# A four-layer decoder on one core: FFN arms reordered, quantised weights turned at other points, tested tiles loaded ahead

## The chip, the core and the metric

The kernel runs on one core of a Trainium2 chip. A core has five engines with instruction queues of their own: TensorE (PE; its weight loads are listed as PEld), VectorE (DVE), ScalarE (ACT), GpSimd (POOL) and SyncE (SP, which here only issues DMAs). TensorE writes PSUM; the others move and change data between PSUM and the on-chip SBUF. The metric is the device time of one execution in microseconds, the median of three runs. Lower is better.

## The reference, cut to what matters

A decoder of four layers works on x of 8 sequences x 112 tokens x 256 features. Each layer has three sublayers (self-attention, cross-attention to a context, feed-forward network), each added to x after a layer norm:

```python
x = x + _L0_ffn_ref(_layernorm(x, axis=-1), L0_ffn_w_gate, L0_ffn_w_up, L0_ffn_w_down)
...
x = x + _L1_ffn_ref(_layernorm(x, axis=-1), L1_ffn_gate_w, L1_ffn_dyn_gate_w, ...)
...
x = x + _L2_ffn_ref(_layernorm(x, axis=-1), L2_ffn_w1_w, L2_ffn_w1_s, L2_ffn_w2_w, ...)
...
x = x + _L3_ffn_ref(_layernorm(x, axis=-1), L3_ffn_gate_w, L3_ffn_up_w, L3_ffn_down_w, ...)
```

Four of the twelve sublayers matter here. Layer 0's FFN is `down(silu(gate(x)) * up(x))` with int32 weights times 1/127 and 768 hidden features. Layer 1's FFN mixes eight small experts and one fixed one by a router. Layer 2's FFN has scaled weights in five products: `silu(w1 x) * (w2 x)` to 1024 features, two further layers h1 and h2 of 1024 x 1024 with a GELU each, and w3 back to 256. Layer 3's FFN fake-quantises its weights to four-bit floats with a scale for each block of 16; the kernel does that quantisation early, beside layer 2's FFN.

## The kernel before

Tokens are worked on in two halves of four sequences (HB = 4, HT = 448 tokens). `self.x` holds x with tokens on partitions, `self.xn` its normed copy, `self.xnT` the normed copy turned, features on partitions, a half in each part of its last axis. A norm is a generator (`normalise`): four pairs of statistics, three groups of small steps for 1/sqrt, two groups that write `xn`, nine steps in all, so that its VectorE work can be dealt out between other work. `turned` puts one 128-feature block of a half through TensorE's transposes.

**Two arms.** The FFNs of layers 0 and 2 have two bodies each, chosen by a flag on the chip. If the weights are exact in a short format, the arm splits every activation into a rounded high part and the rest (`hThi`, `hTlo`, type fp32r) and multiplies both; in the trace both FFNs take this arm. Within an arm the order of TensorE, VectorE and ScalarE is the order of the code (`manual_schedule`); GpSimd's and SP's queues, and all engines between the sublayers, are ordered by a planner at build time, by its own costs and by when inputs are ready.

**One unit of the gated part** is `gated` (line 587): gate and up products for 128 hidden features and one half, 8 matmuls of 128x448 into a `gu` tile (two of these exist), Silu on ScalarE (L595), the product with the up part on VectorE (L597), then `parts` (L571): the high part on ScalarE (L574), the low part, a subtraction, on GpSimd (L576). Scratch for Silu and for the product comes from four pieces of `xnT` (`spare`).

**Layer 0's arm** (`l0_ffn_arm`, lines 1076 to 1092): for each half, turn the half (`turned_parts`, L583 and L585), six gate units with a norm dealt between them, then for each of the four sequences 12 matmuls of 128x256 (six blocks, two parts) and an addition to x (L1092). Layer 1's attention then turns the first half itself (lines 1232 and 1233), computes queries and keys for it, and norms and turns the second half (`ln_T`).

**Layer 1's FFN** tests on the way whether layer 2's weights are exact. `tested(i)` (lines 1470 to 1476) loads one of 11 tiles of 1 MB through SP, two buffers, and takes the sum of magnitudes of the low half words on ScalarE; it is called in the gate units of the second half, in front of other ScalarE work such as the copy of the turned router weights (wT, L1497).

**Layer 2's arm** (`l2_ffn_arm`, lines 2206 to 2249): eight gate units for each half, then h1 and h2: for each half eight units of 16 matmuls of 128x448 (L444), a GELU (L2228), high and low part. Weights come through a ring of four buffers, loaded by GpSimd's DMA queue. Then for each sequence 16 matmuls of 128x256 with w3 and two VectorE steps (L2244, L2245). Beside h1 and h2 the generator `l3_weights` (lines 2484 to 2533) quantises layer 3's three weight tiles: `rounded(i)` is all VectorE work (block maxima L2496, a maximum over partitions on GpSimd L2503, scaling and rounding in two column halves, L2445 to L2478); `turned(i)` puts the result through TensorE (L2520) and copies it (L2521). One step of the generator is taken after unit 3 of each half of h1 and h2; a step turns tile i-1 and rounds tile i. Layer 3's attention (lines 2368 to 2370) then turns the first half itself, and starts a chain: path logits (`paths`), a sigmoid, a product tree (`tree`), turned nodes.

Of the kernel before, what the change touches and what calls it, by code (L numbers as in the profile page):

```python
# [32 lines left out]
P = 128  # L33
# [346 lines left out]
class _Kernel:  # L380
# [190 lines left out]
    def parts(self, dst, src):  # L571

        nc = self.nc
        nc.scalar.copy(dst[0], src)  # L574
        if len(dst) > 1:
            nc.gpsimd.tensor_tensor(dst[1], src, dst[0].bitcast(F32), ALU.subtract)  # L576

    def turned_parts(self, dst, ps, half):

# [4 lines left out]
            if len(dst) > 1:  # L584
                self.nc.vector.tensor_tensor(dst[1][:, kc, cols], tp, dst[0][:, kc, cols].bitcast(F32), ALU.subtract)  # L585

    def gated(self, ps, wg, wu, cols, src, half, dst, scales):

        nc = self.nc
        gu = self.t(ps, [P, 2, 512], "gu")  # L590
        toks = slice(half * HT, (half + 1) * HT)
        for i, m in enumerate((wg, wu)):
            self.mm(gu[:, i, :HT], [(m[:, k, cols], x[:, k, toks]) for k in range(2) for x in src])
        sg = self.spare()
        nc.scalar.activation(sg, gu[:, 0, :HT], AF.Silu, scale=scales[0])  # L595
        h = self.spare() if len(dst) > 1 else dst[0]
        nc.vector.scalar_tensor_tensor(h, gu[:, 1, :HT], scales[1], sg, ALU.mult, ALU.mult)  # L597
        if len(dst) > 1:
            self.parts(dst, h)

    def l0_attn(self):
        nc, tc, w = self.nc, self.tc, self.w
# [455 lines left out]
    def l0_ffn_arm(self, ctx, exact):  # L1058
        nc, tc = self.nc, self.tc
        one = ctx.enter_context(tc.tile_pool(name="l0f_x", bufs=1))  # L1060
        acts = ctx.enter_context(tc.tile_pool(name="l0f", bufs=2))
        ps = ctx.enter_context(tc.tile_pool(name="ps_l0f", bufs=2, space=PSUM))
        ws = []
        for i, (wi, wf) in enumerate(self.wfs):
            if not exact:
                wf = self.t(one, [P, 1536], f"wf{i}")
                nc.gpsimd.tensor_copy(wf, wi)
            ws.append(wf)
        wg, wu = (x.rearrange("p (k n) -> p k n", k=2) for x in ws[:2])
# [6 lines left out]
        hT = {}  # L1076
        for half in range(2):
            hT = self.many(acts, [P, 6, HT], "hT", exact)
            if half:
                self.turned_parts(xT, ps, 1)  # L1080
            for c in range(6):
                dst = [h[:, c, :] for h in hT]
                self.gated(ps, wg, wu, slice(c * P, (c + 1) * P), xT, half, dst, (scale, scale))
                for _ in islice((norm, following)[half], 2):
                    pass
            drain((norm, following)[half])
            for j in range(HB):
                b = half * HB + j
                pm = self.t(ps, [P, 512], "mm")[:S, :D]
                self.mm(pm, [(h[:, c, j * S : (j + 1) * S], wd[:, c, :]) for c in range(6) for h in hT])  # L1090
                x = self.x[:S, b, :]
                nc.vector.scalar_tensor_tensor(x, pm, scale, x, ALU.mult, ALU.add)  # L1092

    def gate_up(self, ps, wg, wu, cols, half):
        gu = self.t(ps, [P, 2, 512], "gu")
# [48 lines left out]
    def l1_attn(self):  # L1144
# [8 lines left out]
        with ExitStack() as ctx:  # L1153
# [75 lines left out]
                oT = oTs.pop(b)  # L1229
                self.add_to_x(b, self.project(ps, b, [oT[:, c, :] for c in range(4)], wo), bo)  # L1230

            for kc in range(2):
                self.cp(self.xnT[:, kc, :HT], self.turned(self.xn, ps, kc, 0, "mm"))
            for c in range(4):
                for which in range(2):
                    query_key(0, c, which)
# [223 lines left out]
    def l1_ffn(self):  # L1460

        nc, tc, w = self.nc, self.tc, self.w
        with ExitStack() as ctx:
            acts = ctx.enter_context(tc.tile_pool(name="l1f", bufs=1))
            work = ctx.enter_context(tc.tile_pool(name="l1f_w", bufs=2))
            test = ctx.enter_context(tc.tile_pool(name="l1f_t", bufs=2))
            ps = ctx.enter_context(tc.tile_pool(name="ps_l1f", bufs=2, space=PSUM))
            low = self.t(acts, [P, len(self.rings["in_wt"][1])], "low")

            def tested(i):  # L1470
                t = self.t(test, [P, COLS], "t")
                nc.sync.dma_start(t, self.args["in_wt"][i])
                bits = t.bitcast(I16).rearrange("p (n two) -> p n two", two=2)[:, :, 0]
                nc.scalar.activation(
                    self.t(test, [P, COLS], "abs", BF16), bits, AF.Abs, accum_out=low[:, i : i + 1]
                )

            self.ln_T(ps)
            route = self.route(ps, acts)
            gw = next(route)  # L1480
# [698 lines left out]
    def l2_ffn_arm(self, ctx, exact):  # L2179

        nc, tc = self.nc, self.tc
        quant = ctx.enter_context(tc.tile_pool(name="l3w", bufs=1))
        acts = ctx.enter_context(tc.tile_pool(name="l2f", bufs=3))
        pool = ctx.enter_context(tc.tile_pool(name="l2f_w", bufs=4))  # L2190
        ps = ctx.enter_context(tc.tile_pool(name="ps_l2f", bufs=2, space=PSUM))
        w = self.ring("in_wt", pool, 4, F32R if exact else F32)
        l3 = iter(self.l3_weights(quant, ps))
        next(l3)

        def block():
            return self.many(acts, [P, 8, HT], "hT", exact)

        xT = [x.rearrange("p (k n) t -> p k (n t)", n=2)[:, :2, :] for x in block()]
        self.turned_parts(xT, ps, 0)  # L2200
        norm = self.normalise(self.x[:, HB:, :], self.xn[:, HB:, :], n=HB)
        w1, w2 = w("w1", 2), w("w2", 2)
        src = []
        for half in range(2):
            dst = block()
            if half:
                self.turned_parts(xT, ps, 1)
            for c in range(8):
                scales = (self.v("l2f_w1_s", c), self.v("l2f_w2_s", c))
                part = [h[:, c, :] for h in dst]  # L2210
                self.gated(ps, w1, w2, slice(c * P, (c + 1) * P), xT, half, part, scales)
                if not half:
                    for _ in islice(norm, 2):
                        pass
            src.append(dst)
        w.done("w2")
        for n in ("h1", "h2"):
            made = []
            for half in range(2):
                dst = block()  # L2220
                for c in range(8):
                    m = w(f"{n}_{c // 2}", 8)
                    pm = self.t(ps, [P, 512], "mm")[:, :HT]
                    cols = slice((c % 2) * P, (c % 2 + 1) * P)
                    self.mm(pm, [(m[:, k, cols], x[:, k, :]) for k in range(8) for x in src[half]])
                    part = [h[:, c, :] for h in dst]
                    y = self.spare() if exact else part[0]
                    nc.scalar.activation(y, pm, AF.Gelu, scale=self.v(f"l2f_{n}_s", c))  # L2228
                    if exact:
                        self.parts(part, y)  # L2230
                    if half and c % 2:
                        w.done(f"{n}_{c // 2}")
                    if c == 3:
                        next(l3, None)
                made.append(dst)
            src = made
        w3, s3 = w("w3", 8), self.o("l2f_w3_s")
        following = self.normalise(self.x[:, :HB, :], self.xn[:, :HB, :], n=HB)
        for b in range(NB):
            toks = slice((b % HB) * S, (b % HB + 1) * S)  # L2240
            pm = self.t(ps, [P, 512], "mm")[:S, :D]
            self.mm(pm, [(h[:, c, toks], w3[:, c, :]) for c in range(8) for h in src[b // HB]])
            y = self.t(quant, [P, D], "y")[:S]
            nc.vector.tensor_tensor(y, pm, s3[:S, :], ALU.mult)  # L2244
            nc.vector.tensor_tensor(self.x[:S, b, :], self.x[:S, b, :], y, ALU.add)  # L2245
            if b >= HB:
                for _ in islice(following, 3):
                    pass
        drain(following)

    def open_last(self, ctx):
        self.w = self.ring("in_wl", ctx.enter_context(self.tc.tile_pool(name="last", bufs=2)), 2)
# [2 lines left out]
    def l3_attn(self):  # L2255
# [10 lines left out]
        with ExitStack() as ctx:  # L2266
# [101 lines left out]
            for kc in range(2):  # L2368
                self.cp(self.xnT[:, kc, :HT], self.turned(self.xn, ps, kc, 0, "mm"))
            paths(0)  # L2370
            tree(0)
            self.ln_T(ps, 1, "mm")
# [111 lines left out]
    def l3_weights(self, pool, ps):  # L2484
# [38 lines left out]
        sizes = ((2, 8), (2, 8), (8, 2))  # L2523
        loaded(0)
        yield
        for i in range(4):
            if i > 0:
                turned(i - 1, *sizes[i - 1])
            if i < 3:
                rounded(i, *sizes[i])  # L2530
            if i < 2:
                loaded(i + 1)
            yield

    def l3_ffn(self):
# [142 lines left out]
```

## Time and profile before

| | us |
|---|---|
| median of three runs | 2171.72 |
| lowest, highest | 2168.49, 2174.79 |
| the profiled execution's own time | 2168.82 |
| its span, first to last instruction | 2167.0 |
| layer 0's arm, first transpose to last sum's start (TensorE) | 536.60 to 585.28 |
| layer 1's attention, first transpose, first query matmul | 587.14, 589.62 |
| layer 1's FFN, second half's gates to the first sums | 947.6 to 998.2 |
| layer 2's gates, first to last matmul's start | 1627.27 to 1663.71 |
| layer 2's h1 and h2 | 1663.90 to 1782.44 |
| layer 2's results | 1782.65 to 1797.57 |
| layer 3's attention, path logits | 1806.31 |

The mean granted clock of TensorE is 0.946 of full speed. The page gives each engine's busy time and its share of the span, then groups of instructions by line, with their mean time and what ended the idle time before them. A timeline line reads: start in us, length in us, engine, line, operation, what it writes and reads, how many; in brackets the idle time before it and what ended that. "issue" is time in which nothing that the profile shows was waited for. Matmuls are pipelined: a 128x448 one in fp32r is listed with 0.36 us, and at full clock one starts every 0.2 us.

### The profile page before, as it was taken

To read this page: it belongs to the slowest core of one execution; us is meant where nothing else is said; L and a number is where in the kernel's file an instruction comes from. 1 tells how busy PE (TensorE), PEld (TensorE's weight loads), DVE (VectorE), ACT (ScalarE), POOL (GpSimd) and SP (SyncE) were. 2 spreads that over 40 slices of the span, in tenths; PEclk is the share of its full clock that TensorE was granted. 3 is DMA by queue.
4 is the path that set the end of the run, shared out by engine and by line. 5 is a ranking of instruction groups with operands and counts; after the bars stand their busy time and mean duration, and the time that the engine had idled before them with its cause. 6 is when DMAs were issued, how large, how long until landed. Compare 5 with 4: busy or idle time off the path is not lost. (4 is left out here: it accounts for less than half of the span.)

```text
span 2167.0 us, 45439 instructions
## 1 busy us (share of the span) xinstructions
PE 1938.5 (89%) x17912; PEld 1244.4 (57%) x17912; DVE 1386.8 (64%) x3905; ACT 869.0 (40%) x2420; POOL 281.9 (13%) x480
## 2 busy tenths in 40 slices
PE   7999999898898899899899989899998997899844
PEld 3545544465666566545566455556667886566623
DVE  5666666686655677553566676567624866667688
ACT  2444444562212456452033223466525322356532
POOL 1111111001302100000001342100003530100000
PEclk9999999998899999999999999999999997999956
DMA  5000001103000000223101010000022210000000
GB/s 208 3 3 3 3 22 39 33 21 107 1 1 16 21 2 2 79 89 135 40 1 59 1 42 8 1 2 2 1 78 72 98 39 26 1 2 2 2 0 17
DMA packets 11486, 69.20 MB, mean 32 GB/s; under 512 B 1290, under 2 KB 3082, under 8 KB 4874
## 3 DMA queue, kind: packets, MB, share of 16 engines
q1 hardware_dynamic: 9684, 54.69, 7.0%
q0 software_dynamic: 1584, 11.54, 1.5%
q8 instruction: 145, 2.38, 0.4%
q14 instruction: 73, 0.60, 0.1%
HBM read 65.30 MB, written 0.92 MB: 31 GB/s over the span
## 5 line engine op out<-in xcount | busy, mean ns | idle before, releaser
L727 PE MATMUL g<-w,hT 128*32 128x256 f32 x3552 | 236.7, 384 | 1.8 <-DVE hT L757 1.5
L1338 DVE TENSOR_REDUCE xnm<-sc 112x1 f32<-112x375 f32 x384 | 184.6, 541 | 40.0 <-PE sc L444 39.4
L1351 PEld LDWEIGHTS tr<-cst,xe 112*125 112x125 f32 x1152 | 151.5, 188 | 94.6 <-issue 38.1
L1351 PE MATMUL tr<-cst,xe 112*125 112x112 f32 x1152 | 192.9, 289 | 6.8 <-DVE xeT L1359 4.2
L727 PEld LDWEIGHTS g<-w,hT 128*32 128x32 f32 x3552 | 93.2, 109 | 121.8 <-DVE hT L757 83.0
L1357 ACT COPY xeT<-tr 125x336 f32<-125x336 f32 x192 | 85.4, 445 | 158.1 <-PE tr L1351 158.1
L444 PE MATMUL mm<-xnT,w 128*128 128x448 f32 x316 | 136.0, 572 | 9.4 <-DVE qT L1320 2.9
L1359 DVE COPY xeT<-tr 125x336 f32<-125x336 f32 x192 | 97.3, 507 | 68.6 <-PE tr L1351 61.8
L690 PE MATMUL g<-xw,cst 128*32 128x256 f32 x1792 | 137.9, 379 | 0.0
L1342 ACT ACTIVATE xe<-sc,xnm 112x375 f32<-112x375 f32 x256 | 126.6, 582 | 7.3 <-DVE xnm L1338 7.3
L753 ACT ACTIVATE th<-cell 128x64 f32<-128x64 f32 x224 | 57.5, 257 | 144.3 <-DVE cell L749 141.9
L444 PE MATMUL mm<-w,hT 128*112 128x256 f32 x448 | 103.4, 392 | 0.0
L740 ACT ACTIVATE sg<-g 128x192 f32<-128x192 f32 x224 | 74.1, 331 | 67.3 <-PE g L727 45.6
L444 PEld LDWEIGHTS mm<-xnT,w 128*128 128x128 f32 x316 | 60.0, 200 | 67.9 <-issue 44.2
L576 POOL TENSOR_TENSOR hTlo<-xnT,hThi 128x448 fp32r<-128x448 f32 x60 | 74.9, 1256 | 160.8 <-issue 82.7
L444 PE MATMUL mm<-hThi,w 128*128 128x448 f32 x256 | 95.2, 372 | 0.0
L444 PE MATMUL mm<-hTlo,w 128*128 128x448 f32 x256 | 94.7, 370 | 0.0
L444 PEld LDWEIGHTS mm<-w,hT 128*112 128x112 f32 x448 | 81.7, 184 | 21.7 <-issue 3.5
L758 POOL COPY hs<-hT 128x16 f32<-128x16 f32 x224 | 51.8, 231 | 318.4 <-DVE hT L757 318.4
L755 DVE TENSOR_TENSOR h<-sg,th 128x64 f32<-128x64 f32 x224 | 50.5, 226 | 63.9 <-ACT th L753 63.8
L444 PE MATMUL sc<-xkT,qT 32*112 32x375 f32 x768 | 89.8, 519 | 0.0
L1367 PE MATMUL av<-xeT,xv 125*32 125x112 f32 x2304 | 86.4, 266 | 2.1 <-ACT xeT L1357 2.1
(482 smaller groups left out, 3961.9 us busy)
## 6 DMA issues: line engine op xcount, KB each, us to landing
w<-in_w SPq DMA_DIRECT2D x22, 1024.0 KB, 5.0
t<-in_wt SPq DMA_DIRECT2D x11, 1024.0 KB, 4.9
w<-in_wt POOLq DMA_DIRECT2D x11, 1024.0 KB, 5.4
raw<-in_wq SPq DMA_DIRECT2D x3, 1024.0 KB, 5.2
cx<-in_ctx SPq DMA_DIRECT2D x2, 1500.0 KB
wi<-in_wint SPq DMA_DIRECT2D x3, 768.0 KB, 5.6
w<-in_w SPq DMA_DIRECT2D x2, 896.0 KB, 10.7
w<-in_w SPq DMA_DIRECT2D x2, 768.0 KB, 4.1
```

The costliest lines, as they stand in the source:

```text
L444: self.nc.tensor.matmul(out, lhsT, rhs, start=i == 0, stop=i == len(pairs) - 1)
L576: nc.gpsimd.tensor_tensor(dst[1], src, dst[0].bitcast(F32), ALU.subtract)
L690: nc.tensor.matmul(g[32 * j : 32 * j + 32, :], pick[:, t % 16, :], xw[:, l, t // 16, 256 * j : 256 * j + 256], start=True, stop=t == 0, sk ...
L727: nc.tensor.matmul(g[32 * j : 32 * j + 32, :], hT[l][:, c, :], whh[l][:, c, 256 * j : 256 * j + 256], start=False, stop=c == 1, skip_group ...
L740: nc.scalar.activation(sg[:, :192], g[:, :192], AF.Sigmoid)
L753: nc.scalar.activation(th, cell[l], AF.Tanh)
L1338: nc.vector.tensor_reduce(nm, sc, AX.X, ALU.max, negate=True)
L1342: nc.scalar.activation(e, sc, AF.Exp, bias=nm)
L1351: nc.tensor.transpose(tp[:CH, i * S : (i + 1) * S], e[:, i * CH : (i + 1) * CH], self.ident[:S, :S])
L1357: nc.scalar.copy(eT, src)
L1359: nc.vector.tensor_copy(eT, src)
L1367: nc.tensor.matmul(avs[b][32 * j : 32 * j + 32, c * S : (c + 1) * S], values[b % 2][:CH, i, 4 * c + j, :], eTs[b, c, j][:, i, :], start=i ...
```

## The change

Layer 0's arm does all six units of the first half, three of the second, the first half's sums, the other three units (with the norm of the new first half dealt between), then the second half's sums over five blocks for four sequences in four PSUM tiles, the next sublayer's transposes of the first half (`head_T`), and last the sixth block. In both arms the low part of every odd unit is subtracted on VectorE instead of GpSimd (`on`). In layer 2's arm the second half is turned after unit 5 of the first; the first half's results are taken after unit 5 of h2's second half, the next norm in units 6 and 7, `head_T` after the sixth result. The generator for layer 3's weights has rounding and turning as steps of their own, taken at units 0 and 7. Layers 1 and 3's attention lose their own transposes of the first half. Tested tiles have three buffers and are loaded three ahead; the tests' output has one buffer of its own.

```diff
-    def gated(self, ps, wg, wu, cols, src, half, dst, scales):
+    def gated(self, ps, wg, wu, cols, src, half, dst, scales, on=None):
...
-            nc.gpsimd.tensor_tensor(dst[1], src, dst[0].bitcast(F32), ALU.subtract)
+            (on or nc.gpsimd).tensor_tensor(dst[1], src, dst[0].bitcast(F32), ALU.subtract)
...
+    def head_T(self, ps):
+
+        for kc in range(2):
+            self.nc.scalar.copy(self.xnT[:, kc, :HT], self.turned(self.xn, ps, kc, 0))
...
+        for _ in units(0, range(6)):
+            for _ in islice(norm, 2):
+                pass
+        drain(norm)
+        self.turned_parts(xT, ps, 1)
+        for _ in units(1, range(3)):
+            pass
+        for j in range(HB):
+            pm = self.t(ps, [P, 512], "mm")[:S, :D]
+            sums(pm, 0, j, range(6))
+            add(pm, 0, j)
+        for _ in units(1, range(3, 6)):
+            for _ in islice(following, 2):
+                pass
+        pms = [self.t(ps, [P, 512], "mm")[:S, :D] for _ in range(2)]
+        wide = self.t(ps, [P, 2, 512], "gu")
+        pms += [wide[:S, i, :D] for i in range(2)]
+        for j in range(HB):
+            sums(pms[j], 1, j, range(5))
+        drain(following)
+        self.head_T(ps)
+        for j in range(HB):
+            sums(pms[j], 1, j, (5,))
+            add(pms[j], 1, j)
...
-            for kc in range(2):
-                self.cp(self.xnT[:, kc, :HT], self.turned(self.xn, ps, kc, 0, "mm"))
...
-            test = ctx.enter_context(tc.tile_pool(name="l1f_t", bufs=2))
+            test = ctx.enter_context(tc.tile_pool(name="l1f_t", bufs=3))
+            junk = ctx.enter_context(tc.tile_pool(name="l1f_j", bufs=1))
...
+                loaded()
+
+            for _ in range(3):
+                loaded()
...
+                on = nc.vector if c % 2 else nc.gpsimd
+                self.gated(ps, w1, w2, slice(c * P, (c + 1) * P), xT, half, part, scales, on)
                 if not half:
                     for _ in islice(norm, 2):
                         pass
+                    if c == 5:
+                        drain(norm)
+                        self.turned_parts(xT, ps, 1)
...
                 for c in range(8):
+                    if c in (0, 7):
+                        next(l3, None)
...
-                    if c == 3:
-                        next(l3, None)
+                    if n == "h2" and half:
+                        if c == 5:
+                            for b in range(HB):
+                                result(b, made[0])
+                        if c > 5:
+                            for _ in islice(following, 4):
+                                pass
...
         drain(following)
+        for b in range(HB, NB):
+            result(b, src[1])
+            if b == HB + 1:
+                self.head_T(ps)
...
-        for i in range(4):
-            if i > 0:
-                turned(i - 1, *sizes[i - 1])
-            if i < 3:
-                rounded(i, *sizes[i])
+        for i in range(3):
+            rounded(i, *sizes[i])
             if i < 2:
                 loaded(i + 1)
+            yield
+            turned(i, *sizes[i])
             yield
```

More of the change, by code (lines that the diff above doesn't have):

```diff
@@ L569, in spare, with parts @@
         return self.xnT[:, self.turn // 2, (self.turn % 2) * HT : (self.turn % 2 + 1) * HT]
-    def parts(self, dst, src):
+    def parts(self, dst, src, on=None):
         nc = self.nc
@@ L598, in gated @@
         if len(dst) > 1:
-            self.parts(dst, h)
+            self.parts(dst, h, on)
+    def head_T(self, ps):
+        for kc in range(2):
+            self.nc.scalar.copy(self.xnT[:, kc, :HT], self.turned(self.xn, ps, kc, 0))
     def l0_attn(self):
@@ L1075, in l0_ffn_arm @@
         following = self.normalise(self.x[:, :HB, :], self.xn[:, :HB, :], n=HB)
[L1076 to L1092, printed above, removed]
+        hT = [self.many(acts, [P, 6, HT], "hT", exact) for _ in range(2)]
@@ new lines, in units, with sums @@
+        def units(half, cs):
+            for c in cs:
+                dst = [h[:, c, :] for h in hT[half]]
+                on = nc.vector if c % 2 else nc.gpsimd
+                self.gated(ps, wg, wu, slice(c * P, (c + 1) * P), xT, half, dst, (scale, scale), on)
+                yield
+        def sums(pm, half, j, cs):
+            for c in cs:
+                for h in hT[half]:
+                    nc.tensor.matmul(
+                        pm, h[:, c, j * S : (j + 1) * S], wd[:, c, :],
+                        start=c == 0 and h is hT[half][0], stop=c == 5 and h is hT[half][-1], skip_group_check=True,
+                    )
@@ new lines, in add @@
+        def add(pm, half, j):
+            x = self.x[:S, half * HB + j, :]
+            nc.vector.scalar_tensor_tensor(x, pm, scale, x, ALU.mult, ALU.add)
+        for _ in units(0, range(6)):
[9 more added lines that the diff above has]
+            add(pm, 0, j)
@@ L1465, in l1_ffn, with loaded @@
             work = ctx.enter_context(tc.tile_pool(name="l1f_w", bufs=2))
-            test = ctx.enter_context(tc.tile_pool(name="l1f_t", bufs=2))
+            test = ctx.enter_context(tc.tile_pool(name="l1f_t", bufs=3))
+            junk = ctx.enter_context(tc.tile_pool(name="l1f_j", bufs=1))
             ps = ctx.enter_context(tc.tile_pool(name="ps_l1f", bufs=2, space=PSUM))
             low = self.t(acts, [P, len(self.rings["in_wt"][1])], "low")
+            raws = []
+            def loaded():
+                if len(raws) < low.shape[1]:
+                    raws.append(self.t(test, [P, COLS], "t"))
+                    nc.sync.dma_start(raws[-1], self.args["in_wt"][len(raws) - 1])
             def tested(i):
-                t = self.t(test, [P, COLS], "t")
-                nc.sync.dma_start(t, self.args["in_wt"][i])
-                bits = t.bitcast(I16).rearrange("p (n two) -> p n two", two=2)[:, :, 0]
+                bits = raws[i].bitcast(I16).rearrange("p (n two) -> p n two", two=2)[:, :, 0]
                 nc.scalar.activation(
-                    self.t(test, [P, COLS], "abs", BF16), bits, AF.Abs, accum_out=low[:, i : i + 1]
+                    self.t(junk, [P, COLS], "abs", BF16), bits, AF.Abs, accum_out=low[:, i : i + 1]
                 )
+                loaded()
+            for _ in range(3):
+                loaded()
             self.ln_T(ps)
@@ L2205, in l2_ffn_arm @@
             dst = block()
-            if half:
-                self.turned_parts(xT, ps, 1)
             for c in range(8):
@@ L2210, in l2_ffn_arm @@
                 part = [h[:, c, :] for h in dst]
-                self.gated(ps, w1, w2, slice(c * P, (c + 1) * P), xT, half, part, scales)
+                on = nc.vector if c % 2 else nc.gpsimd
+                self.gated(ps, w1, w2, slice(c * P, (c + 1) * P), xT, half, part, scales, on)
                 if not half:
@@ L2214, in l2_ffn_arm, with result @@
                         pass
+                    if c == 5:
+                        drain(norm)
+                        self.turned_parts(xT, ps, 1)
             src.append(dst)
         w.done("w2")
+        s3 = self.o("l2f_w3_s")
+        following = self.normalise(self.x[:, :HB, :], self.xn[:, :HB, :], n=HB)
+        def result(b, src):
+            w3 = w("w3", 8)
+            toks = slice((b % HB) * S, (b % HB + 1) * S)
+            pm = self.t(ps, [P, 512], "mm")[:S, :D]
+            self.mm(pm, [(h[:, c, toks], w3[:, c, :]) for c in range(8) for h in src])
+            y = self.t(quant, [P, D], "y")[:S]
+            nc.vector.tensor_tensor(y, pm, s3[:S, :], ALU.mult)
+            nc.vector.tensor_tensor(self.x[:S, b, :], self.x[:S, b, :], y, ALU.add)
         for n in ("h1", "h2"):
@@ L2232, in l2_ffn_arm @@
                         w.done(f"{n}_{c // 2}")
-                    if c == 3:
-                        next(l3, None)
+                    if n == "h2" and half:
[5 more added lines that the diff above has]
+                                pass
                 made.append(dst)
             src = made
[L2237 to L2248, printed above, removed]
         drain(following)
+        for b in range(HB, NB):
+            result(b, src[1])
+            if b == HB + 1:
+                self.head_T(ps)
     def open_last(self, ctx):
@@ L2366, in result @@
                 self.add_to_x(b, self.project(ps, b, [oT[:, c, :] for c in range(2)], wo))
-            for kc in range(2):
-                self.cp(self.xnT[:, kc, :HT], self.turned(self.xn, ps, kc, 0, "mm"))
             paths(0)
@@ L2525, in l3_weights @@
         yield
-        for i in range(4):
-            if i > 0:
-                turned(i - 1, *sizes[i - 1])
-            if i < 3:
-                rounded(i, *sizes[i])
+        for i in range(3):
+            rounded(i, *sizes[i])
             if i < 2:
                 loaded(i + 1)
+            yield
+            turned(i, *sizes[i])
             yield
```

## The prediction

> **What bounds the kernel now.** I read the page first, then the chain of work that ended last in the stretches that the diff touches, then each engine's timeline there.
>
> ```profile
> PE 1938.5 (89%) x17912; PEld 1244.4 (57%) x17912; DVE 1386.8 (64%) x3905; ACT 869.0 (40%) x2420; POOL 281.9 (13%) x480
> ```
>
> TensorE is busy nearly always, and the change neither adds nor removes a matmul. So only TensorE's idle time in the four touched stretches can be won or lost, and the slow matmuls that follow idle time. The largest such wait is in layer 2's FFN. In the chain there (start, length, piece):
>
> ```profile
> 1704.40 1.15 POOL hTlo L576
> ...
> 1705.79 6.00 issue
> ...
> 1711.86 0.39 POOL gs L2503
> ...
> 1720.17 1.53 DVE wq L2478
> 1721.70 1.07 DVE qs L2445
> 1722.80 3.52 DVE qs L2446
> ...
> 1737.83 1.46 PE tr L2520 x12
> 1739.30 28.20 PE mm L444 x128
> ```
>
> Here rounding matrix 1 on VectorE (1704.69 to 1737.78, 33.1 us) took longer than the 8 units (one half of an h layer) that TensorE had in front of it, and TensorE waited from 1730.1 to 1737.83: 7.7 us. Two things stretch the rounding. GpSimd is gone for 6.00 us ahead of its partition reduction (0.39 us), and VectorE's small steps are held while GpSimd subtracts (L2446 took 3.52 us here, 0.20 where GpSimd was away). VectorE's timeline for matrix 0:
>
> ```profile
> 1665.89 3.72 DVE L2496 TENSOR_REDUCE amax<-raw 128x128 f32<-128x2048 f32 x1
> ...
> 1677.38 0.16 DVE L2504 RECIPROCAL gs<-gs 128x1 f32<-128x1 f32 x1 [7.45 <-POOL gs L2503]
> ```
>
> It ended at 1701.81, 35.9 us after its start, and no one waited: its turning stood at unit 12.
>
> The other waits are short. TensorE in the sums of layer 0's FFN, and at the heads of the layers behind both arms:
>
> ```profile
> 552.93 0.37 PE L444 MATMUL mm<-wf,hThi 128*112 128x256 f32 x1 [0.61 <-ACT hThi L574]
> 554.14 0.37 PE L444 MATMUL mm<-wf,hTlo 128*112 128x256 f32 x1 [0.84 <-POOL hTlo L576]
> ...
> 587.14 0.96 PE L515 MATMUL mm<-cst,xn 112*128 112x112 f32 x8 [1.59 <-DVE st L480]
> ```
>
> ```profile
> 1800.47 0.99 PE L515 MATMUL mm<-cst,xn 112*128 112x112 f32 x8 [2.63 <-DVE y L2244]
> 1806.31 3.21 PE L444 MATMUL mm<-own,xnT 128*112 128x40 f32 x16 [4.85 <-DVE xnT L437]
> ```
>
> **1. Turning the quantised weights: +15.8.** Count TensorE's units of h1 and h2 from 0, 16 matmuls each at 0.2025 us, 3.24 us, unit 0 starting at 1663.90. Before, rounding 0 is issued at unit 3, turning 0 at unit 12, turning 1 at 20, turning 2 at 28. After, the two steps are separate and are taken at c = 0 and c = 7 of each half: rounding 0 at unit 0, turning 0 ahead of unit 7, rounding 1 at unit 8, turning 1 at 15, turning 2 at 23. VectorE has no other work in these units, so rounding 0 cannot start sooner for being issued sooner; its turning stands five units earlier.
>
> Rounding 0, from 1663.90: it started at 2.0; the last unit's subtraction, now on VectorE in front of it, makes that 3.3. Its two reductions take 4.04, so the maximum is ready at 7.35. GpSimd subtracts for unit 0 until 7.27 (1671.17), then is gone 5.8 us and reduces; VectorE goes on at 13.5, as before. The steps left need 16.7 us when nothing holds them (8.6 for the first column half, 1677.38 on, less its two held steps; 8.1 for the second). GpSimd comes back at 20.4 (1684.29) with six subtractions waiting; before, seven took VectorE 6.2 us, so six take 5.3. End: 13.5 + 16.7 + 5.3 = 35.5. TensorE is at unit 7 at 22.9 (1686.8) and in order, so everything behind waits **12.6 us**. After the 7.7 us wait before, 12 transposes and 14 matmuls took 6.4 us where full speed needs 3.5: **2.9** more.
>
> Rounding 1 then finds GpSimd drained, as matrix 2 did before (26.3 us, reduction waited for 0.55): start 37.8, end 64.1; TensorE needs 1.4 + 8 x 3.24 + 2.3 and is at unit 15 at 65.2: no wait, by 1 us. Rounding 2 finds GpSimd just having subtracted, as matrix 1 did before: 67.2 + 33.1 = 100.3, TensorE at unit 23 at 92.0: **8.3**, plus 2.9. Sum 26.7 against 7.7 + 2.9 before, and 0.3 for the four transposes that could run ahead of that wait: +15.8. Bounds: with no gap at the reduction and no held steps rounding 0 lasts 21.3 us, ends at 24.6, and the first wait is 1.7; with none later, the sum is 9 below before. With matrix 1 late as well (33.1 or more), another 6 to 11 above. Where GpSimd's queue puts the reduction is not in the diff; I take the order that the trace shows, by when inputs are ready.
>
> **2. Layer 0's arm: -2.9.** I lay the arm out from its rows: gate unit 8 x 0.2015; Silu 0.55, product 0.62 (L597), high part 0.57, low part 1.15 on GpSimd; a norm 2.2 us of statistics, 2.2 of small steps, 1.5 of scaling. A low part on VectorE has no row; the subtraction L585 of that shape took 0.62. Bounds: 0.2 below (64-element steps) and 1.15 above, if a GpSimd subtraction holds it (L463 took 1.12 instead of 0.16); I take 0.62.
> Gone, counted between issues: the waits in both sums (0.77 + 1.09 + 0.44 + 1.10, twice: 6.8), the half-speed matmuls after them (17 at 0.213 instead of 0.118, twice: 3.2), 1.1 at the half boundary, 0.9 at unit 5 of half 1: 12.0. New: VectorE waits at odd units for the high part, subtracts, and only then takes norm steps, +1.2 in half 0. The transposes of half 1 now come straight behind unit 5: they wait 2.3 for the norm, and the next gates wait 2.1 for casts that stand behind unit 5's on ScalarE (the same order cost 2.4 between issues at 1647.33), 1.6 of half-speed matmuls follow. At the end 1.9 for unit 4's GpSimd part, 0.9 for the next norm, 0.75 for transposes moved in, 0.8 for an even chance of slow matmuls: 11.6. So -0.4 in the arm. Behind it 585.56 to 589.62 (4.06) shrinks to 1.58, as the head's transposes are done: -2.5. Bounds -6 (no slow matmuls) and +2 (the first query evacuations queue behind the other half's 6 us norm).
>
> The Trainium skill (TensorE: Matmul & The Clock Gate, What's actually happening) has the clock fall only after an idle window of about 3.4 us; here 2.2 us idle was followed by 8 slow matmuls (1648.58 on). By the page the boundary would cost 1.6 less; I go by the row. The same skill (SBUF — State Buffer, Who interferes with whom) says that a VectorE instruction with two SBUF inputs and a GpSimd one that reads SBUF block each other; that speaks against half the subtractions on VectorE, and would put the sum about 1 us higher, as an estimate; the L463 row shows such a hold. The sum does not use it.
>
> **3. Layer 2's gates: -0.5.** The same layout with 0.63 and 0.68: half 1's transposes now come behind unit 5 and hide most of the 2.9 us between issues at the boundary, but norm and low parts on VectorE delay half 0 by 1.1 and the transposes by 2.2, and half 1's loop grows 0.1 a unit. Bounds -2 and +1.5 (the slow matmuls stay or not).
>
> **4. Layer 2's end: -3.8.** The first half's results run ahead of unit 6, so the last unit's parts are no longer covered: low part 2.6 us after its matmuls, 1.65 of sums in front, +0.8; transposes +0.8. Behind the arm the path head came 8.46 after the last matmul (1797.85 to 1806.31); now TensorE needs about 2.5. Then z, sigmoid, tree, with VectorE shared with the other half's norm: tree end 17.4 before, about 12 after: -5.4. Bounds -6 and -1 in all (norm last, norm first). w3, now read three units sooner, is issued by GpSimd at unit 1 of that half, lands in 5.4 us and is read at unit 5, 13 us later: nothing.
>
> **5. Tested tiles: -1.3.** TensorE waits 5.20 for wT behind three tests on ScalarE; one of them waited 1.27 for its tile. Three tiles loaded at the start remove that; the rest stays. The other wait (1.56) has no TensorE wait behind it: nothing. The loads are issued by SP in the same places, one more at the start, where the DMA engines are mostly idle; the tests' shared output is written by ScalarE alone, in order, and costs nothing. SP also issues the raw weights, 5.2 us to land, two steps ahead of their use: nothing. Bounds 0 and -2.
>
> **Sum:** 15.8 - 2.9 - 0.5 - 3.8 - 1.3 = +7.3. The profiled execution took 2168.82 (span 2167.0); the median is 2.9 higher. 2171.72 + 7.3 = **2179.0**.
>
> **Rivals.** (a) GpSimd reduces ahead of unit 0's subtraction: its gap starts some 3 us sooner and fewer steps are held, first wait about 7: 2173, within 0.3% (what a measurement here can tell from nothing, 6.5 us). For it: the reduction is issued first now. Against: the trace orders by readiness, and unit 0's part is ready at 6.0, the maximum at 7.35. (b) Rounding 1 is late too, as its margin is 1 us: +11, 2190. (c) Faster: GpSimd's gap is hidden and few steps held in all three roundings, so part 1 is 9 under before, and parts 2 to 5 keep 8.5: 2154. It decides when the three roundings stay below 24 us; the shortest so far was 26.3. (d) It does not do what it says: the weights are not turned later against TensorE, and part 1, at about half of its size, cancels parts 2 to 5: 2171.
>
> **Numbers.** Forecast 0.50 (2174 to 2184, of it 0.10 below 2178.2), (a) 0.18, (b) 0.15, (c) 0.12, (d) 0.05. Faster 0.12, same 0.10 + 0.18 + 0.05 = 0.33, slower 0.40 + 0.15 = 0.55. The range takes in (a), (b) and (d), with part 2's better end: 2165 to 2192.
>
> **What would show it.** TensorE's longest wait in h1 and h2 on the rounded weights (wq, L2478) in front of unit 7 of h1, about 12 us, then none, then about 8. Waits of 2 us on the norm and the casts between layer 0's halves; no waits on hThi or hTlo in its first sums; the attention's first matmul about 1.6 behind the arm. It is wrong if the first wait is under 5 us, or the chain passes elsewhere.

## The result and the profile after

| us | before | after |
|---|---|---|
| median, 14 runs each, on the same chip | 2169.04 | 2174.66 |
| lowest, highest | 2167.29, 2174.79 | 2171.15, 2182.90 |
| the profiled execution, its span | 2168.82, 2167.0 | 2173.44, 2171.5 |
| layer 0's arm, first transpose to first query product | 53.0 | 52.3 |
| layer 2's gates, first matmul to the first of h1 | 36.6 | 34.3 |
| first matmul of h1 to the path logits | 142.4 | 150.0 |

The changed kernel is slower by 0.22% (ratio 1.0022, 95% interval 1.0013 to 1.0031). The forecast was 2179.0 and slower by over 0.3%; the time lies in its range, but in the case "within 0.3%".

The page's busy times of the changed kernel:

```profile
PE 1935.5 (89%) x17912; PEld 1241.9 (57%) x17912; DVE 1389.4 (64%) x3917; ACT 869.4 (40%) x2422; POOL 262.9 (12%) x466
```

The number of matmuls is the same; GpSimd has lost 19 us and 14 subtractions, VectorE has gained 12 instructions. Next the list of TensorE's waits (who waits for whom: us in all, times, longest), the touched ones. Lines of the code have moved: L2529 was L2478, L2571 was L2520.

```profile
PE tr L2571 <- DVE wq L2529: 19.4, 2, 10.1
PE tr L444 <- ACT wT L1537: 4.4, 2, 3.8
```

Before, these were 7.7 (one wait) and 5.8 (longest 5.2). The rounded weights are waited for twice instead of once. VectorE's and GpSimd's timelines show the first rounding:

```profile
1664.62 3.73 DVE L2547 TENSOR_REDUCE amax<-raw 128x128 f32<-128x2048 f32 x1
...
1672.16 0.17 DVE L2555 RECIPROCAL gs<-gs 128x1 f32<-128x1 f32 x1 [3.49 <-POOL gs L2554]
...
1682.35 1.14 DVE L2496 TENSOR_SCALAR qs<-amax,gs 128x64 f32<-128x64 f32 x1
1683.52 1.08 DVE L2497 TENSOR_SCALAR qs<-qs 128x64 f32<-128x64 f32 x1
```

```profile
1662.28 1.14 POOL L576 TENSOR_TENSOR hTlo<-xnT,hThi 128x448 fp32r<-128x448 f32 x1 [0.59 <-ACT hThi L574]
...
1671.74 0.38 POOL L2554 PARTITION_ALL_REDUCE gs<-top  x1 [7.79 <-issue]
1678.88 8.93 POOL L576 TENSOR_TENSOR hTlo<-xnT,hThi 128x448 fp32r<-128x448 f32 x7 [6.76 <-issue]
```

GpSimd goes to the reduction ahead of unit 0's subtraction, is gone 7.79 us before it and 6.76 after it, and comes back with seven subtractions due; beside them five of VectorE's steps of 64 elements take 1.05 to 1.14 us instead of 0.20 to 0.23. The rounding lasts 30.2 us, and TensorE waits:

```profile
1694.89 1.46 PE L2571 MATMUL tr<-ident,wq 128*128 128x128 bf16 x12 [10.09 <-DVE wq L2529]
1696.12 0.72 PE L444 MATMUL mm<-hThi,w 128*128 128x448 f32 x1
1696.64 0.57 PE L444 MATMUL mm<-hTlo,w 128*128 128x448 f32 x1
```

A matmul listed with 0.57 runs at half speed (0.37 us to the next one). TensorE's timeline between layer 0's halves, behind its arm, between layer 2's halves, and at layer 2's end:

```profile
553.37 0.55 PE L515 MATMUL tr<-cst,xn 112*128 112x112 f32 x2 [0.59 <-DVE xn L490]
554.46 1.02 PE L515 MATMUL tr<-cst,xn 112*128 112x112 f32 x6 [0.54 <-DVE xn L490]
556.87 0.74 PE L444 MATMUL gu<-xThi,wf 128*128 128x448 f32 x1 [1.39 <-ACT xThi L583]
```

```profile
585.99 0.27 PE L1093 MATMUL gu<-wf,hTlo 128*112 128x256 f32 x1
589.23 3.33 PE L444 MATMUL mm<-xnT,w 128*128 128x448 f32 x4 [2.96 <-DVE va L455]
```

```profile
1642.09 1.02 PE L515 MATMUL tr<-cst,xn 112*128 112x112 f32 x6 [0.60 <-DVE xn L490]
1642.88 0.45 PE L444 MATMUL gu<-hThi,w 128*128 128x448 f32 x1
```

```profile
1809.92 0.28 PE L444 MATMUL mm<-w,hTlo 128*112 128x256 f32 x1
1811.45 0.75 PE L444 MATMUL mm<-own,xnT 128*112 128x40 f32 x6 [1.24 <-DVE x L2269]
```

Behind waits of 0.56 and 0.60 us ahead of the transposes, the gates of layer 2's second half start without one (before, 2.22 us and half speed behind it). The first query product stands 3.24 us behind layer 0's arm (before 4.3), though its operand is ready; the path logits stand 1.5 us behind layer 2's (before 8.7).

### The profile page after: what moved, and what is told of

It reads as the page before. It is cut to its first block, busy times and chain, and to the rows that moved or that the text cites. A ratio compares the mean times of both kernels' runs of the same rounds, so it can differ in the third digit from the quotient of the medians.

```text
span 2171.5 us, 45439 instructions
## 1 busy us (share of the span) xinstructions
PE 1935.5 (89%) x17912; PEld 1241.9 (57%) x17912; DVE 1389.4 (64%) x3917; ACT 869.4 (40%) x2422; POOL 262.9 (12%) x466
## 5 line engine op out<-in xcount | busy, mean ns | idle before, releaser
L1398 PEld LDWEIGHTS av<-xeT,xv 125*32 125x32 f32 x2304 | 58.6, 109 | 43.1 <-issue 34.6
## 6 DMA issues: line engine op xcount, KB each, us to landing
w<-in_w SPq DMA_DIRECT2D x2, 896.0 KB, 10.8
```

What stands on the lines that cost most here:

```text
L1398: nc.tensor.matmul(avs[b][32 * j : 32 * j + 32, c * S : (c + 1) * S], values[b % 2][:CH, i, 4 * c + j, :], eTs[b, c, j][:, i, :], start=i ...
```

## The experiments

Executions of one kernel differ by several us in code that no edit touched (TensorE falls to half speed at other places), so beside each median stand the stage's times from the profiled execution. "h1 to paths" is from the first matmul of h1 to the path logits. In this stage the same code took 150.0 us (changed), 151.8 (e12) and 152.6 (e6), so a difference under some 3 us there says little by itself. The ratio is to the kernel before, timed beside each run.

| kernel | median | ratio to before, 95% interval | gates | h1 to paths |
|---|---|---|---|---|
| before | 2169.0 to 2169.8 | | 36.6 | 142.4 |
| changed | 2174.66 | 1.0013 to 1.0031 | 34.3 | 150.0 |
| e1, old points | 2160.96 | 0.9951 to 0.9979 | 34.3 | 137.3 |
| e2, before with the new points | 2184.97 | 1.0052 to 1.0091 | 36.7 | 158.6 |
| e3, points 0, 11, 21, 31 | 2160.92 | 0.9940 to 0.9972 | 34.3 | 135.6 |
| e4, no reduction | 2162.59 | 0.9949 to 0.9982 | 34.3 | 138.5 |
| e5, no subtractions in h1, h2 | 2158.35 | 0.9935 to 0.9964 | 34.3 | 132.4 |
| e6, old layer 0 | 2177.31 | 1.0020 to 1.0046 | 34.3 | 152.6 |
| e7, points 0, 11, 22, 31 | 2158.51 | 0.9933 to 0.9959 | 34.3 | 131.6 |
| e8, low parts on GpSimd | 2174.82 | 1.0004 to 1.0031 | 33.2 | 151.2 |
| e9, e7 and e8 | 2156.07 | 0.9928 to 0.9960 | 33.2 | 138.6 |
| e10, before with e7's points | 2172.72 | 1.0007 to 1.0029 | 36.7 | 143.5 |
| e11, old end | 2183.91 | 1.0044 to 1.0070 | 34.3 | 156.3 |
| e12, old boundary | 2181.08 | 1.0040 to 1.0064 | 37.7 | 151.8 |

My theory: the points at which the weights are turned cost about 13 us, everything else gains. The main rival: the points cost little, the loss sits in layers 0 and 1.

**e1: the old points in the changed kernel**, with the old generator, which turns matrix i-1 and rounds matrix i in one step.

```diff
-                    if c in (0, 7):
-                        next(l3, None)
...
+                    if c == 3:
+                        next(l3, None)
```

> The changed kernel with the old points for the quantised weights (one step of the generator after unit 3 of each half; a step turns matrix i-1, then rounds matrix i); all else as changed. Theory T (the turning points cost what the two profiles show: h1 and h2 without the moved results took 118.7 us before and 131.9 after, so 13.2; everything else gains): 2174.7 - 13 = 2161 to 2162, faster than both kernels; one wait of TensorE on the rounded weights, 7 to 8 us, instead of 10.1 and 9.3. Rival R (the turning points cost little on balance, because the slow matmuls and the rounding contention come anyway, and the loss sits in layers 0 and 1): 2170 to 2175.

Measured 2160.96, 13.7 less than the changed kernel, and 12.7 less from h1 to the paths. The rival falls. One wait is left:

```profile
PE tr L2571 <- DVE wq L2529: 7.2, 1, 7.2
```

**e2: the new points in the kernel before.**

```diff
-        for i in range(4):
-            if i > 0:
-                turned(i - 1, *sizes[i - 1])
-            if i < 3:
-                rounded(i, *sizes[i])
+        for i in range(3):
+            rounded(i, *sizes[i])
...
+            yield
+            turned(i, *sizes[i])
...
+                    if c in (0, 7):
+                        next(l3, None)
...
-                    if c == 3:
-                        next(l3, None)
```

> The kernel before with only the new points for the quantised weights (rounding at unit 0, turning at unit 7 of a half, as steps of their own). Theory T: 2169.0 + 13 = 2182 (waits of TensorE on the rounded weights of about 10 ahead of unit 7 of h1 and 9 ahead of unit 7 of h2's first half, each followed by slow matmuls). My prediction on record put this part at +15.8, so 2185. Rival R: 2169 to 2174.

2184.97: 15.2 more than the kernel before, 16.2 in the stage. The recorded +15.8 is near this sum, but not by its terms: TensorE's waits on the rounded weights were 10.10, 0.71 and 9.54 us, where it had 12.6, none and 8.3, and one of 1.53 on the GELU's scratch came on top. That the errors cancel is luck.

**e3: later points**, with the old generator.

```diff
-                    if c in (0, 7):
+                    if (n, half, c) in (("h1", 0, 0), ("h1", 1, 3), ("h2", 0, 5), ("h2", 1, 7)):
                         next(l3, None)
```

> The changed kernel with the generator's steps (turn i-1, round i) at units 0, 11, 21 and 31 of h1 and h2, so that each rounding has 10 or 11 units of TensorE (32 to 36 us) in front of its turning. Theory T (a rounding takes 27 to 35 us of VectorE; a turning less than that behind its rounding is a wait, one that is further behind costs nothing): no wait on the rounded weights, the two waits of 19.4 and about 5 of slow matmuls behind them gone: 2174.7 - 24 = 2151, faster than the kernel before by 18. Rival R2 (three roundings back to back end at about 100 us, where the moved results begin, and VectorE holds their sums): the wait moves there, 2157 to 2163.

2160.92, neither theory's mechanism. The third rounding ended at 1768.4, before the moved results; the second one was late:

```profile
1700.51 3.70 DVE L2547 TENSOR_REDUCE amax<-raw 128x128 f32<-128x2048 f32 x1
...
1711.85 0.16 DVE L2555 RECIPROCAL gs<-gs 128x1 f32<-128x1 f32 x1 [7.32 <-POOL gs L2554]
```

It lasted 38 us (27.2 in the changed kernel, where its reduction was waited for 0.55), and TensorE waited 4.57 for it. In the changed kernel TensorE's own 10 us of standing had left GpSimd without subtractions, so that it had changed over to the reduction in time:

```profile
1701.16 0.38 POOL L2554 PARTITION_ALL_REDUCE gs<-top  x1 [13.35 <-DVE top L2553]
```

With no such wait the change-over came late. The other traces agree: in each kernel that subtracts and reduces, a rounding behind a wait of TensorE of 4.6 us or more waited 0.55 or 0.56 for its reduction, and one behind a shorter wait or none 1.5 to 7.9. My theory took the length of a rounding as a given; it depends on the wait that it causes.

**e4: no reduction.**

```diff
-            nc.gpsimd.partition_all_reduce(gs, top, P, bass_isa.ReduceOp.max)
+            nc.vector.tensor_copy(gs, top)
```

> The changed kernel with the maximum over partitions left out (each partition's own maximum is used, so the scale of the quantised weights is another); a copy of one element a partition on VectorE stands in its place. GpSimd then only subtracts. Theory G (both things stretch a rounding: the wait for the reduction, 3.5, 0.6 and 7.6 us in the three, and small steps held by GpSimd's subtractions): roundings of about 27 us each, the waits of 10.1 and 9.3 shrink to about 6.6 and 2: 2174.7 - 12 = 2163. Rival G2 (the holds come only in a burst when GpSimd returns from the reduction with 6 or 7 subtractions due; without a gap there is no burst): roundings of 22 to 24 us, waits 2 and 0: 2174.7 - 21 = 2154. Rival G3 (VectorE alone sets the length): less than 4 us gained, 2171 or more.

2162.59, waits of 5.48 and 1.31 us: theory G. What is left of the two waits is then to come from the subtractions that hold VectorE, which e5 takes away.

**e5: no subtractions in h1 and h2.**

```diff
                     if exact:
-                        self.parts(part, y)
+                        for d in part:
+                            nc.scalar.copy(d, y)
```

> The changed kernel, but in h1 and h2 the low part is a copy of the whole value on ScalarE (so the products there are other ones) and GpSimd subtracts nothing beside the roundings; it keeps the three maxima over partitions and the weight loads. Theory G (GpSimd pays 6 to 7 us each time it goes from subtractions to the maximum and back, and its subtractions hold VectorE's small steps): with no subtraction between them the second and third maximum are waited for 0.6 us, no step is held, and roundings take about 21 to 22 us where the reduction is not waited for; the two waits of TensorE shrink from 10.1 and 9.3 to at most 3 and 0: 2174.7 - 19 = 2156. Rival G4 (the 6 to 7 us belong to every maximum over partitions by itself, whatever stands before it): the second and third are waited for about 7 us too, roundings of 28 us, waits of about 8 and 3: 2165.

2158.35; waits of 3.97 and none. The second rounding, which waits for nothing, lasts 21.2 us (1691.37 to 1712.55), and no step of 64 elements is held. GpSimd's timeline:

```profile
1672.27 0.38 POOL L2555 PARTITION_ALL_REDUCE gs<-top  x1 [7.90 <-issue]
1695.49 0.35 POOL L2555 PARTITION_ALL_REDUCE gs<-top  x1 [22.84 <-DVE top L2554]
...
1724.28 0.35 POOL L2555 PARTITION_ALL_REDUCE gs<-top  x1 [0.94 <-DVE top L2554]
```

Only the first reduction, behind the gates' subtractions, has the gap; the other two run as soon as VectorE has their input, weight loads between them or not. So the gap ahead of a reduction belongs to the change from subtractions (theory G; G4 falls). The gap on the way back, 6.7 to 7.7 us ahead of the first subtraction behind each reduction, is missing in e4, which has no reduction.

**e6: layer 0's old arm** in the changed kernel.

```diff
-        hT = [self.many(acts, [P, 6, HT], "hT", exact) for _ in range(2)]
...
+        hT = {}
+        for half in range(2):
+            hT = self.many(acts, [P, 6, HT], "hT", exact)
...
+            for kc in range(2):
+                self.cp(self.xnT[:, kc, :HT], self.turned(self.xn, ps, kc, 0, "mm"))
```

> The changed kernel with layer 0's old arm, and layer 1's attention turning its first half itself as before; the rest as changed. My prediction on record put layer 0's part at -2.9, so without it 2177.6. Theory S (the gain in the arm is given back at once: the first query product waits 2.96 us for VectorE behind the arm, and the matmuls behind that wait run at half speed): 2174 to 2175.5. Rival S2 (the new arm is a loss, and the profile of one execution hides it): 2172 or less.

2177.31: 2.7 more, which is the recorded number and not theory S. But the two intervals overlap (1.0013 to 1.0031, 1.0020 to 1.0046), and the profiles give 0.5 up to the first query product (0.7 against the kernel before) and nothing at the attention's next transposes, at 609 us. Between -1 and 6 us is all that the times say.

**e7: e3 with the second turning one unit later.**

```diff
-                    if (n, half, c) in (("h1", 0, 0), ("h1", 1, 3), ("h2", 0, 5), ("h2", 1, 7)):
+                    if (n, half, c) in (("h1", 0, 0), ("h1", 1, 3), ("h2", 0, 6), ("h2", 1, 7)):
```

> The changed kernel with the generator's steps at units 0, 11, 22 and 31. With 0, 11, 21 and 31 it took 2160.9; TensorE waited there 4.57 us ahead of the second turning, and slow matmuls followed. Theory T: one unit (3.24 us) later leaves a wait of 1.3 and no slow matmuls: 2160.9 - 3.3 - 2.5 = 2155, faster than both kernels. Rival R2 (the third rounding then reaches into the moved results and VectorE holds their sums): no gain, 2160 to 2162.

2158.51, faster than both kernels, by less than expected. A wait of 1.36 on the rounded weights is left, 1.45 on the GELU's scratch and 1.48 on the sums:

```profile
1720.45 0.47 PE L444 MATMUL mm<-hThi,w 128*128 128x448 f32 x1 [1.45 <-ACT xnT L2284]
```

**e8: every low part on GpSimd**, in both arms.

```diff
-                on = nc.vector if c % 2 else nc.gpsimd
+                on = nc.gpsimd
```

> The changed kernel with every low part of the two arms on GpSimd, as before; all else as changed. By my prediction VectorE's share of them delays the first half's gates (1.2 us in layer 0, 1.1 in layer 2, and the transposes behind unit 5 by 2.2), against waits for GpSimd at the sums and at the end of the arms. Theory V (the gates gained 2.3 us through the place of the transposes alone, and VectorE's subtractions cost a little): layer 2's gates 33 to 34 us instead of 34.3, time 2173 to 2175. Rival V2 (taking half the subtractions from GpSimd is what keeps the arms free of waits): 2177 to 2180, with waits on the low parts in layer 0's sums of the first half.

2174.82, the same. Layer 2's gates are 1.1 shorter, as theory V has it, and layer 0 to the first query product is 47.8 instead of 52.3; h1 to the paths is 1.2 longer. In e9, with the same low parts, layer 0 takes 48.4; the other kernels with the new arm take 50.9 to 52.7. So by these two profiles the new order of layer 0 gains 4.6 to 5.2 us on the kernel before (53.0), and the low parts on VectorE take most of that away. The medians don't show it: e8's 12 runs spread from 2164 to 2179, and where its 4.5 us are lost again stays open.

**e9: e7's and e8's edits together.**

> The changed kernel with the generator's steps at units 0, 11, 22 and 31 (2158.5 by itself) and every low part on GpSimd (which by itself made layer 2's gates 33.2 us instead of 34.3 and took 2174.8 against 2174.7). Theory V (VectorE's subtractions lengthen the gates by 1.1 us in layer 2 and by about as much in layer 0, and the later first rounding that this brings is now covered): 2158.5 - 2 = 2156 to 2157. Rival: nothing that these runs can tell, 2158 to 2160.

2156.07, the lowest median of all; its interval overlaps e7's, so the time doesn't show theory V. From h1 to the paths it took 7.1 us more than e7 (in an execution whose earlier layers took 13 us less): the sums waited 3.02 us for VectorE and then ran at half speed for 6.1, and a second wait for the scratch was enough for half speed:

```profile
1709.57 0.54 PE L444 MATMUL mm<-hThi,w 128*128 128x448 f32 x1 [1.76 <-ACT xnT L2284]
1709.91 0.58 PE L444 MATMUL mm<-hTlo,w 128*128 128x448 f32 x1
```

**e10: e7's points in the kernel before**; the edit is e7's line in place of `if c == 3`.

> The kernel before with nothing changed but the generator's steps, at units 0, 11, 22 and 31 in place of 3, 12, 20 and 28. Theory T: the wait of 7.7 us and the 2.9 of slow matmuls go, a wait of 1 to 2 stays: 2169.3 - 9 = 2160. With the arms' parts added it took 2158.5, so these would then be worth less than the 8.8 that they showed with the old points. Rival (h1 and h2 last 112.7 us without the moved results there and 118.5 before, so 5.8 and no more): 2163.5.

2172.72, slower than before: the expectation fell, and its rival too. TensorE no longer waits 7.7 us for the rounded weights, but it waits elsewhere:

```profile
1684.65 0.74 PE L444 MATMUL mm<-hThi,w 128*128 128x448 f32 x1 [2.83 <-ACT xnT L2230]
```

```profile
1674.66 0.38 POOL L2503 PARTITION_ALL_REDUCE gs<-top  x1 [8.06 <-issue]
1682.50 7.41 POOL L576 TENSOR_TENSOR hTlo<-xnT,hThi 128x448 fp32r<-128x448 f32 x6 [7.45 <-issue]
```

The GELU writes into one of four scratch pieces, which are free again when GpSimd has subtracted from them. Here GpSimd is back 20.3 us behind the start of h1 (1662.21), when TensorE has done six units; in e7 after 17.3 (1662.75 to 1680.03). With 1.47 more for the scratch, 1.34 and 1.76 for the rounded weights, the 7.7 us are spent again: h1 and h2 last 119.4 us, before 118.5. In e7 the same two rows are:

```profile
1672.60 0.38 POOL L2554 PARTITION_ALL_REDUCE gs<-top  x1 [7.34 <-issue]
1680.03 8.70 POOL L576 TENSOR_TENSOR hTlo<-xnT,hThi 128x448 fp32r<-128x448 f32 x7 [7.05 <-issue]
```

Of the 3.0 us by which GpSimd is back sooner in e7, 1.9 come from the last gate unit's low part on VectorE: GpSimd's last subtraction began at 1663.58, 0.83 behind h1's start, here at 1664.95, 2.74 behind it. The other 1.1 lie in the gaps, which are shorter in e7; why is open. e9 fits: every low part on GpSimd, its last subtraction 2.75 behind h1's start, back after 19.2, a wait of 1.61 for the scratch.

**e11: the old end of layer 2's arm** in the changed kernel.

```diff
-                    if n == "h2" and half:
-                        if c == 5:
-                            for b in range(HB):
-                                result(b, made[0])
...
-        for b in range(HB, NB):
-            result(b, src[1])
-            if b == HB + 1:
-                self.head_T(ps)
+        for b in range(NB):
+            result(b, src[b // HB])
+            if b >= HB:
+                for _ in islice(following, 3):
+                    pass
```

> The changed kernel with the old end of layer 2's arm: all eight results behind h2, the next norm dealt between the last four, the next attention turning its first half itself. My prediction on record put this part at -3.8, so without it 2178.5. By the profiles (from the first matmul of h1 to the path logits, the old points gave 142.4 us with the old end and 137.3 with the new one): 5.1, 2179.8. Rival (the first half's results inside h2 delay the third turning or its rounding): below 2176.

Measured 2183.91, 9.2 more than the changed kernel, with 156.3 us from h1 to the paths against 150.0. Only part of these 6.3 us lies at the end: without the first half's sums, which take 7.4 there in the changed kernel, h1 and h2 lasted 134.7 and 131.6 us, though e11 doesn't touch them (TensorE waited 1.84 for the second rounding and 1.15 for the scratch). The touched end itself is 3.2 longer.

**e12: the old boundary of layer 2's halves** in the changed kernel.

```diff
+            if half:
+                self.turned_parts(xT, ps, 1)
             for c in range(8):
...
-                    if c == 5:
-                        drain(norm)
-                        self.turned_parts(xT, ps, 1)
```

> The changed kernel with layer 2's second half turned between the halves, as before, and the low parts of odd units still on VectorE. My prediction put the moved transposes and the low parts together at -0.5. Theory V (the transposes' place is worth 3.5: no wait of 2.2 us for casts, no half-speed matmuls behind it; the low parts cost 1.1): gates of 37.5 to 38 us instead of 34.3, time 2174.7 + 3.5 = 2178. By my prediction: gates of 35 to 35.5, 2175.5.

In e12 the boundary is as it was before the change:

```profile
1650.48 0.47 PE L444 MATMUL gu<-hThi,w 128*128 128x448 f32 x1 [2.14 <-ACT hThi L583]
```

2181.08, 6.4 more than the changed kernel. The gates are 3.4 longer; 1.8 of the rest stand from h1 to the paths, which e12 doesn't touch. So both parts gain: the new end 3.2 by e11's profile and 5.1 by e1's against the kernel before, around the 3.8 that I had put down, and the place of the transposes 3.4, more than I had put down. What the medians show above that is not explained.

## Why the prediction was right and wrong

| step | predicted | stages of the profiles | medians |
|---|---|---|---|
| 1 turning | +15.8 | +12.7 (alone +16.2) | +13.7 (alone +15.2) |
| 2 layer 0's arm | -2.9 | -0.7 to 0 | -2.7, unsure |
| 3 layer 2's gates | -0.5 | -2.3 | transposes alone -6.4 |
| 4 layer 2's end | -3.8 | -5.1 (with the new points -3.2) | -9.2 |
| 5 tested tiles | -1.3 | -1.4 | not tried alone |
| sum | +7.3 | +3.2 to +3.9 | +5.6 (all together) |

Together, parts 2 to 5 were put at -8.5; e1 against the kernel before gives -8.8. Taken singly, the medians of parts 2 to 4 (2.7, 6.4 and 9.2) add to 18.3, more than their intervals explain easily. Some of it is other code: e11 and e12 were also slower in h1 and h2, by 3.1 and 1.8 us in the profiles. The rest stays open.

**The step that failed is the first wait of part 1**, "TensorE is at unit 7 at 22.9 (1686.8) and in order, so everything behind waits 12.6 us", with 2.9 of slow matmuls behind each wait. The wait was 10.1, so this term of the sum was 2.5 too large: the reduction stood ahead of unit 0's subtraction, so VectorE waited 3.49 us for it, where I had 13.5 - 7.35 = 6.2, and went on 10.7 behind h1's start instead of 13.5. That is rival (a)'s order; but (a)'s wait of 7 was not reached, since seven subtractions came in one burst and held VectorE for 6.0 us (22.7 from there to the end, less 16.7; I had 5.3 for six). The slow matmuls cost 2.2 behind the first wait and some 0.8 behind the second, whose 16 transposes already ran through half of the slow time. With 9.3 for 8.3 in the other wait: 19.4 + 3.0 - 7.7 - 2.9 = 11.8, against 15.8 on record and 12.7 in the stage.

That the whole came near, +5.6 for +7.3, is in part luck: part 1's loss was put too high by about 3 and part 2's gain by 2 to 3, while part 3 gained 1.8 more than put down, so that errors of both signs cancel. Of the 4.3 us between 2179.0 and 2174.66, 2.7 come from the base: three runs of the kernel before had given 2171.72, fourteen gave 2169.04.

- Second rounding: hidden, "by 1 us". In the changed kernel's profile it just was: its transposes began at 1723.89 without a wait, and it ended at 1724.18. With the same points it was late by 0.71 us in e2, 0.91 in e6 and 1.84 in e11. That is rival (b)'s condition, but at a small part of its price of 11.
- Part 2: the arm's own balance was -0.4 on record and +0.4 by the trace (48.7 to 49.1 us). Behind it the step failed: not 1.58 but 3.24 us, a wait until VectorE had finished the statistics of the other half. The waits at the boundary were 0.59, 0.54 and 1.39, and the half speed behind them cost about 3 us where I had 1.6 (16 matmuls took 6.5 us). The low parts on VectorE, put at 1.2 in half 0, cost 4.5 in all by e8's profile. No waits in the first sums: right.
- Part 3: I let the boundary's waits come back behind unit 5. The transposes waited 0.56 and 0.60, the gates behind them not at all, and no matmul ran at half speed. The low part on VectorE took 0.63 as assumed, and the 1.1 for it is what e8 shows.
- Part 4: 1.5 us from the last sum to the path logits, where I had 2.5, and the tree ended 10.1 us behind the last matmul (17.4 before), where I had about 12.
- Part 5: 3.81 instead of 5.20; e2, with the old loads, has 5.8 for that wait and e1 3.8.
- Rival (c) did not come: no rounding of this kernel was under 27 us; e5's 21.2 show what it would have needed.

## What to carry to other kernels

A moved wait is priced with the engine that feeds its producer: here the time that TensorE stood was the time in which GpSimd could change over, so taking the wait away made the next rounding longer (27 to 38 us) and let the scratch run out. Where an engine alternates between two kinds of work with a dear change-over, count how much is queued behind each change, and give the consumer the whole length of the producer plus one unit: e7 did that and is 10.8 us faster than the kernel before. Before a new order is judged as a whole, try its parts: here one part cost 13.7 and the others gained 8.8.

## What the runs showed of the hardware

- GpSimd's change-over: 5.8 to 8.7 us, mostly listed as "issue", ahead of a reduction that follows subtractions, and 6.7 to 7.7 ahead of the next subtraction; none between reductions (e5). The Trainium skill (GPSIMD Engine Reference, Instruction dispatch) gives about 6 us for the first call to a freshly loaded kernel; here a gap of that size stands at each change, in both directions, where the reduction's input isn't late enough to cover it. Whether it is the same cost no run here shows.
- Half speed after short waits: in h1 and h2, waits for the GELU's scratch of 1.15 to 1.61 us (six rows) were followed by full speed, 1.76, 1.94 and 2.83 by 3.0 to 3.3 us at half speed. Elsewhere the length of the wait alone doesn't decide: ahead of the second turning 0.71 to 1.84 us (e2, e6, e7, e10, e11) were followed by full speed, ahead of the third 1.31 (e4) and 1.76 (e10) by half speed, behind transposes with further small waits. The Trainium skill (TensorE: Matmul & The Clock Gate, What's actually happening) puts the fall behind an idle window of about 3.4 us; by these rows the clock also falls where no single wait is that long.
- The first query product behind layer 0's arm waited in every kernel with the new arm (2.96 to 3.46 us) until VectorE had done the next norm's first steps, which it doesn't read. Why the wait is released so late is open; no run here takes it apart.
